# A graph layer's partial sums: sixteen of 37 additions moved from VectorE to a ScalarE copy and an accumulating transfer

## The chip, the core and the metric

The kernel runs on one core of a Trainium2 chip. The metric is the time of one execution on the device in microseconds (us); three runs of the kernel before gave a median of 516.62 us. The profile is of a further execution of its own. TensorE (PE) multiplies matrices into PSUM, VectorE (DVE), ScalarE (ACT) and GpSimd (POOL) work on tiles in SBUF and PSUM, and SyncE (SP) issues transfers. "PEld" is TensorE's loading of weights, which runs beside its matmuls.

## What is computed

A graph layer and then a mixture of experts. The graph layer normalizes the 2,048 rows of x (256 wide), gathers a row for each of 67,584 edges, scales it by the edge's weight, sums the scaled rows by the edge's other end, and adds the sums and a value of each node to x. The experts' layer (eight experts, two for each row) follows and needs all of these sums.

```python
def _L0_gnn_ref(x, values, indices, bias):
    row = indices[0]
    col = indices[1]
    gathered = values[:, None] * x[col]
    out = jax.ops.segment_sum(gathered, row, num_segments=OUT_FEATURES)
    return out + bias
...
edge_index = jnp.stack([src, dst])
x = x + _L0_gnn_ref(_layernorm(x, axis=-1), edge_weight, edge_index, node_vec1)
x = x + _L0_ffn_ref(_layernorm(x, axis=-1)[None], L0_ffn_Wr, L0_ffn_br, L0_ffn_ln_g, L0_ffn_ln_b, L0_ffn_W1, L0_ffn_b1, L0_ffn_W2, L0_ffn_b2)[0]
```

## The kernel before

The kernel turns the edges into a dense matrix of 2,048 x 2,048 and multiplies it by the normalized rows. The rows lie in SBUF in 16 blocks of 128: "acc" holds x and becomes the result, 264 floats a row (256 and eight sums for the later routing); "xn" holds the normalized rows.

The edge loop (a loop over n from 0 to 31, called steps here) makes the dense matrix, 64 columns a step:

- VectorE compares the edges' keys with a counting row: `make_hl` (L330, tile "hl"), `make_eq` (L337, "eq") and `make_hr` (L345, "hr"). It does this one step ahead: step n makes the tiles of step n + 1. "hl" and "hr" have two buffers each.
- `make_cols` multiplies them on TensorE (96 matmuls, L369) into two PSUM tiles "pa" a step, out of a pool of three, and ScalarE copies each to "ar" (L372). SP sends "ar" to a tensor "ad" in DRAM and, after every second step, reads the finished block back as "ac" (L373, L376).
- From step 8 on, `dense` (L383) multiplies finished blocks by the normalized rows, for one pair of row blocks a step, into a PSUM tile "py1" out of a pool of two. The blocks come in groups, `GROUPS`: blocks 0 to 2 for steps 8 to 15, blocks 3 to 6 for steps 16 to 23, blocks 7 to 10 for steps 24 to 31. Blocks 11 to 15 follow after the loop.
- `add` (L388) adds the pair of one step to "acc" in the step after it, on VectorE, after that step's "hl", "eq" and "hr".

Every fourth step a new window of edges is prepared. At steps 1, 5, 9, 13, 17 and 21 `get_win` computes an index on VectorE (L239, L240) and GpSimd gathers three windows (L244, "win_s", "win_d", "win_w"), and, up to step 13, `get_run` another piece of the list (L225, "run"). At steps 4, 8 and so on up to 24 `turn_keys` transposes keys "f" on TensorE (L295, L300), ScalarE copying each before the next (L296, L302). `next_part` splits the weights further two steps later (VectorE L321, ScalarE L322). `X_WORK` is a list of ScalarE's work on x with the step of each item: squares (L429), normalizing (L449) and adding the node values (L454); it ends at step 14. `count_before` (L234) and `scale_dst` (L282) are ScalarE's too.

All of this is inside `tc.manual_schedule`: the instructions of each engine stay in the order in which they are written, so the order within a step is the one of the loop's body. An engine that waits for a semaphore holds up all that stands behind it. Each of GpSimd's transfers is written by GpSimd itself, in its order.

These lines of the loop's body set the order around the change:

```python
elif n % 4 == 1 and q + 2 < GQ:
    get_win(q + 2)
    if q + 4 < GQ:
        get_run(q + 4)
...
for p in late:
    add(*p)
late = []
make_cols(n, *hots.pop(n))
g, k = divmod(n - NB // 2, NB // 2)
if g >= 0:
    late.append(dense(GROUPS[g], 2 * k))
```

Of the kernel before, what the change touches and what calls it, by code (L numbers as in the profile page):

```python
# [10 lines left out]
F32 = mybir.dt.float32  # L11
# [4 lines left out]
OP = mybir.AluOpType  # L16
# [6 lines left out]
P = 128  # L23
# [4 lines left out]
def kernel(  # L28
# [30 lines left out]
    nc = tc.nc  # L59
# [3 lines left out]
    NB = N // P  # L63
# [23 lines left out]
    DX = D + NE  # L87
# [11 lines left out]
    acc = consts.tile([P, NB, DX], F32, name="acc")  # L99
# [11 lines left out]
    pool = lambda name, bufs, **k: edges.enter_context(tc.tile_pool(name=name, bufs=bufs, **k))  # L111
# [148 lines left out]
    hotl = pool("hotl", 2)  # L260
    hotr = pool("hotr", 2)
    rowsp = pool("rowsp", 3)
    ps_k = pool("ps_k", 1, space=PSUM)
    ps_a = pool("ps_a", 3, space=PSUM)
    two = lambda t, g, n: t[:, g * GH:(g + 1) * GH, None, :].to_broadcast([P, GH, n // 2, 2])
# [120 lines left out]

    def add(b, pa):
        nc.vector.tensor_add(acc[:, b:b + 2, :], acc[:, b:b + 2, :], pa[:, :, :DX])  # L388

    ads, acs = {}, {}  # L390
    ET = mybir.EngineType
    ALL = {ET.DVE, ET.Pool, ET.PE, ET.Activation, ET.SP}
    with tc.manual_schedule(engines=ALL):
# [104 lines left out]
        for n in range(NH):  # L498
# [22 lines left out]
            if n in (5, 9, 11):  # L521
                b = {5: 4, 9: 8, 11: 12}[n]
                scales_x(slice(b, b + 4))
            if n in (6, 10, 12):
                b = {6: 0, 10: 4, 12: 8}[n]
                weigh_n(slice(b, b + (8 if n == 12 else 4)))
            for p in late:
                add(*p)
            late = []
            make_cols(n, *hots.pop(n))  # L530
            g, k = divmod(n - NB // 2, NB // 2)
# [58 lines left out]
        for p in range(NA // 2):  # L590
            late.append(dense(GROUPS[3], 2 * p))
            add(*late.pop(0))
        add(*late.pop(0))
    edges.close()

# [7 lines left out]
    with tc.If(n_used < E):  # L603
# [15 lines left out]
        with tc.tile_pool(name="any", bufs=2) as anyp, tc.tile_pool(  # L619
            name="ps_any", bufs=2, space=PSUM  # L620
# [544 lines left out]
    with ExitStack() as nest:  # L1165
        for u in range(SURE - 2, len(whole)):
            s = whole[u]
# [46 lines left out]
```

## Time and profile before

| | |
|---|---|
| median of three runs | 516.62 us (516.45 to 517.64) |
| profiled execution, its own time | 517.81 us |
| its span, first to last instruction | 516.0 us |
| mean granted TensorE clock | 0.967 |
| busy: PE, DVE, ACT, POOL | 460.1, 280.2, 198.5, 153.0 us |
| additions on VectorE (L388) | 37, 25.8 us busy, 700 ns each |
| edge loop with block matmuls (L383 beside L369) | about 74 to 206 us of the span |

A page of the profile gives the busy time of each engine and its groups of instructions. Idle time before a group is put down to what ended it. The busy shares are means over the whole span; a stage is read from its own stretch, and the timeline gives the start and length of the instructions in it. In the timeline, instructions of one kind in a row are merged ("x2"), and what is in brackets is the idle time before and what ended it. The clock column is the share of full TensorE clock that was granted.

### The profile page before, as it was taken

Reading aid. Unit: us, or ns where it says so; the run is one execution under the profiler, and the core shown is the slowest. Engines: PE = TensorE matmul, PEld = TensorE weight load, DVE = VectorE, ACT = ScalarE, POOL = GpSimd, SP = SyncE. Lnnn points to the kernel's source line nnn. Section 1 sums busy time; section 2 is a strip of 40 time slices with the busy share of each in tenths; the row PEclk is TensorE's granted clock in tenths of the full one; section 3 lists DMA queues with packets and bytes.
Section 4 is the critical chain, followed back from the end, with each engine's and each line's share of the span. In section 5 each row is a group of like instructions: output and inputs, shape, how many; then the busy total and the mean of one; then the engine's idle time right before and its main releaser. Section 6 shows DMA issues by size and latency. Waiting matters only on the chain.

```text
span 516.0 us, 12139 instructions
## 1 busy us (share of the span) xinstructions
PE 460.1 (89%) x4996; PEld 390.7 (76%) x4996; DVE 280.2 (54%) x582; ACT 198.5 (38%) x479; POOL 153.0 (30%) x127
## 2 busy tenths in 40 slices
PE   0665898888999999989999999999999999997993
PEld 0454676667877787878887888888888888886882
DVE  5979499999999994247847222243333222121011
ACT  2456386673323321048382332323333333332220
POOL 5470205060330000000142444544343344422231
PEclk9978589999999999999999999999999999999898
DMA  7345556877666566893513996799998667739420
GB/s 230 90 152 140 165 180 215 247 247 211 193 201 207 193 203 191 283 316 109 176 52 83 304 337 199 219 355 375 344 334 287 175 174 214 214 71 332 133 99 31
DMA packets 87684, 106.82 MB, mean 207 GB/s; under 512 B 8656, under 2 KB 77376, under 8 KB 85504
## 3 DMA queue, kind: packets, MB, share of 16 engines
q1 hardware_dynamic: 78576, 91.03, 54.5%
q0 software_dynamic: 7952, 13.77, 11.4%
q10 hardware_dynamic: 1088, 1.09, 0.6%
q8 instruction: 44, 0.72, 0.5%
q14 instruction: 24, 0.20, 0.1%
HBM read 79.85 MB, written 28.14 MB: 209 GB/s over the span
## 4 chain that ended last, share of the span: by engine, by line
PE 43%; DMA 10%; issue 1%; DVE 1%; SPq 0%; POOL 0%; POOLq 0%; DVEq 0%
PE py L1045 17%; PE ph L1031 17%; DMA xs<-xr_d,to_i 7%; PE py L383 4%; PE px L858 2%; DMA out<-y_d 1%; PE px L996 1%; DMA y_rows<-out,to_i 1%; DMA out<-ys,to_i 0%; SPq L1183 0%; PE listed L839 0%; POOL out L1066 0%; POOLq L1210 0%; DVE in_hi L831 0%; DVE in_lo L825 0%
## 5 line engine op out<-in xcount | busy, mean ns | idle before, releaser
L1031 PE MATMUL ph<-xeT,w 128*128 128x256 f32 (+1 forms) x576 | 123.9, 372 | 5.7 <-PEq L1171 4.1
L1031 PEld LDWEIGHTS ph<-xeT,w 128*128 128x128 f32 x576 | 105.1, 192 | 20.6 <-issue 7.2
L1045 PE MATMUL py<-w,hT 128*128 128x256 f32 x544 | 120.6, 379 | 0.0
L1033 ACT ACTIVATE hT<-ph,ec 128x256 f32<-128x256 f32 (+1 forms) x144 | 65.7, 461 | 137.6 <-PE ph L1031 80.1
L1045 PEld LDWEIGHTS py<-w,hT 128*128 128x128 f32 x544 | 102.0, 190 | 13.2
L383 PE MATMUL py<-xn_lo,ac 128*128 128x264 f32 x352 | 85.6, 396 | 0.0
L1053 POOL DMA_INDIRECT y_d<-ys,to_i x30 | 48.9, 1630 | 115.1 <-DVE ys L1048 81.1
L330 DVE TENSOR_TENSOR hl<-k,iota_b 128x4096 bf16<-128x4096 bf16 x32 | 73.1, 2285 | 9.4 <-PE pa L369 9.1
L383 PEld LDWEIGHTS py<-xn_lo,ac 128*128 128x128 f32 x352 | 65.5, 192 | 12.7 <-ACT xn_lo L449 0.2
L369 PE MATMUL pa<-hl,hr 128*32 128x128 bf16 x3072 | 59.4, 234 | 12.2 <-DVE hr L345 6.3
L369 PEld LDWEIGHTS <-hr 128*32 128x32 bf16 x3072 | 49.8, 104 | 24.7 <-issue 14.6
L1048 DVE SCALAR_TENSOR_TENSOR ys<-py,wt,b2w 128x256 f32<-128x256 f32 x34 | 16.4, 484 | 80.6 <-PE py L1045 66.1
L345 DVE TENSOR_TENSOR hr<-eq,w 128x3072 bf16<-128x3072 bf16 x32 | 56.3, 1758 | 2.0 <-ACT w L322 0.5
L963 POOL DMA_INDIRECT xs<-xr_d,to_i x40 | 41.8, 1044 | 52.4 <-DVE r L729 32.8
L1005 DVE TENSOR_SCALAR xeT<-px,ec 128x256 f32<-128x256 f32 (+1 forms) x38 | 18.4, 526 | 63.4 <-PE px L996 55.5
L372 ACT COPY ar<-pa 128x512 f32<-128x512 f32 x64 | 35.6, 585 | 38.6 <-PE pa L369 26.6
L244 POOL DMA_INDIRECT win_s<-in_src,at_i x8 | 11.7, 1458 | 94.7 <-DVE at_i L240 46.2
L388 DVE TENSOR_TENSOR acc<-acc,py 128x528 f32<-128x528 f32 x37 | 25.8, 700 | 22.2 <-PE py L383 22.2
L383 PE MATMUL py<-xn_hi,ac 128*128 128x264 f32 x160 | 36.2, 387 | 1.4 <-DVEq L603 1.4
L383 PEld LDWEIGHTS py<-xn_hi,ac 128*128 128x128 f32 x160 | 30.2, 190 | 6.8 <-issue 1.8
L1020 ACT ACTIVATE b2w<-b,wt 128x256 f32<-128x256 f32 x36 | 16.3, 499 | 27.8 <-DVE wt L1018 25.6
L337 DVE TENSOR_TENSOR eq<-k,iota_b 128x1024 bf16<-128x1024 bf16 x32 | 21.9, 685 | 0.0
(208 smaller groups left out, 331.4 us busy)
## 6 DMA issues: line engine op xcount, KB each, us to landing
w<-in_L_ffn_W SPq DMA_DIRECT2D x44, 1024.0 KB
ad<-ar SPq DMA_DIRECT2D x32, 512.0 KB
ac<-ad SPq DMA_DIRECT2D x16, 1024.0 KB
b<-in_L_ffn_b SPq DMA_DIRECT2D x22, 128.0 KB
out<-y_d SPq DMA_DIRECT2D x4, 512.0 KB
xr_d<-rec SPq DMA_DIRECT2D x1, 1300.0 KB
y_d<-acc SPq DMA_DIRECT2D x1, 1280.0 KB
acc<-in_x SPq DMA_DIRECT2D x2, 512.0 KB
```

The lines of the kernel that those rows point to most:

```text
L330: nc.vector.tensor_tensor(hl.rearrange("p g (n t) -> p g n t", t=2), two(k2[:, 0], g, P), pair(P), OP.is_equal)
L337: nc.vector.tensor_tensor(eq.rearrange("p g (n t) -> p g n t", t=2), two(k2[:, 1], g, RK), pair(RK), OP.is_equal)
L345: nc.vector.tensor_tensor(hr.rearrange("p g i (n t) -> p (g i) n t", t=2), eq[:, :, None, :].to_broadcast([P, GH, 3, RK]), w[:, :, None, : ...
L369: nc.tensor.matmul(pa[j * RK:(j + 1) * RK, m, :], hr[:, g, i, :], hl[:, g, :], start=(i == 0), stop=(i == 2), tile_position=(0, j * RK))
L372: nc.scalar.copy(ar[:, m0:m0 + 4, :], pa)
L383: nc.tensor.matmul(pa[:, i, :DX], acs[c][:, b + i, :], xn(c), start=(c == blocks[0]), stop=(c == blocks[-1]))
L388: nc.vector.tensor_add(acc[:, b:b + 2, :], acc[:, b:b + 2, :], pa[:, :, :DX])
L963: nc.gpsimd.indirect_dma_start(out=(sets[s.set][0] if into is None else into)[:, t, :], out_offset=None, in_=(xr_d if rows is None else ro ...
L1031: nc.tensor.matmul(ph, w1[:, k, c * P:(c + 1) * P], xeT[:, k, :], start=(k == 0), stop=(k == KD - 1))
L1033: nc.scalar.activation(hT[:, c, :s.n * P], ph, AF.Gelu, bias=ec[:, c:c + 1], scale=1.0)
L1045: nc.tensor.matmul(py, hT[:, c, t * P:(t + 1) * P], w2[:, c, :], start=(c == 0), stop=(c == KH - 1))
L1053: st = nc.gpsimd.indirect_dma_start(out=y_d[:, :], out_offset=bass.IndirectOffsetOnAxis(ap=tos[s.to][:, t:t + 1], axis=0), in_=ys, in_offs ...
```

## The change

A pool "sums" with two buffers of 128 x 2 x 264 floats is added. A second function, `add_far`, copies the PSUM pair to such a buffer on ScalarE and then issues a transfer from GpSimd that adds the buffer to the rows of "acc" in SBUF. The loop uses it for the pairs that are added at steps 9 to 16 (those of the first group) and at every odd step after; the even steps from 18 on and all additions after the loop keep `add`.

```diff
+    sums = pool("sums", 2)
...
     def add(b, pa):
         nc.vector.tensor_add(acc[:, b:b + 2, :], acc[:, b:b + 2, :], pa[:, :, :DX])
+
+    def add_far(b, pa):
+
+        s = sums.tile([P, 2, DX], F32, name="sum")
+        nc.scalar.copy(s, pa[:, :, :DX])
+        nc.gpsimd.dma_start(acc[:, b:b + 2, :], s, accum_op=OP.add)
...
             for p in late:
-                add(*p)
+                (add_far if n <= NB or n % 2 else add)(*p)
```

## The prediction

> **What bounds the kernel now.** I call a turn n of the edge loop "step n". I read first where the sums stand, then who waits for them. The table of stretches, for steps 9 to 20 (columns: busy us and instruction count of PE, PEld, DVE, ACT, POOL, then clock, DMA share, GB/s):
>
> ```profile
> 80.00:102.00 22.00, 19.80 (x511) 15.75 (x514) 21.69 (x30) 13.74 (x40) 8.55 (x4) 1.00 0.73 216
> 102.00:124.00 22.00, 19.31 (x407) 15.01 (x399) 21.72 (x24) 12.57 (x31) 8.16 (x4) 1.00 0.73 220
> 124.00:146.00 22.00, 21.18 (x438) 17.16 (x424) 21.72 (x24) 7.62 (x19) 5.39 (x3) 1.00 0.78 241
> ```
>
> VectorE has no gap in any of them. TensorE has some in the first two and hardly any in the third: three block matmuls a row block become four at step 16, and from there TensorE is full as well. So what VectorE loses is worth at most TensorE's gaps before step 17. The waits of PE from 80 to 124 us size them:
>
> ```profile
> PE pa L369 <- issue: 1.4, 3, 0.5
> PE pk L295 <- DVE f L276: 1.1, 2, 0.7
> PE pk L300 <- ACT k L296: 0.9, 2, 0.5
> PE pk L295 <- ACT k L296: 0.5, 1, 0.5
> PE pk L295 <- DVE acc L388: 0.5, 1, 0.5
> PE pa L369 <- DVE hr L345: 0.3, 1, 0.3
> ```
>
> Only waits on VectorE can go. In the timeline of PE they are three holes, worked out from start to start: 0.79 us before step 12's transposes, 0.37 before step 16's edge matmuls, 0.47 before step 16's transposes; 1.63 us in all. The row on "acc" is really the round trip through ScalarE (0.46, like its neighbours) and stays; so do the issue gaps. After step 17 I compared, step by step, the end of hr on VectorE with the start of the matmuls that use it: 1.8, 1.6 and 1.3 us at steps 18 to 20, still 1.9 at step 28 and 0.4 at step 31. TensorE always takes it later. The eight sums moved there are worth nothing.
>
> **What is removed.** Sixteen additions leave VectorE, eight at steps 9 to 16 and eight at odd steps 17 to 31. From the timeline of DVE:
>
> ```profile
> 81.93 0.70 DVE L388 TENSOR_TENSOR acc<-acc,py 128x528 f32<-128x528 f32 x1
> 82.54 2.28 DVE L330 TENSOR_TENSOR hl<-k,iota_b 128x4096 bf16<-128x4096 bf16 x1
> ```
>
> Start to start is 0.61 us, so 16 x 0.61 = 9.8 us of VectorE, of which 1.6 us can show in the time.
>
> **What is added on ScalarE.** Sixteen copies of 128x528 from PSUM. The nearest row is the copy of 128x512 from PSUM at L372, 585 ns, so 0.55 to 0.6 us each, 9.3 us in all. ScalarE is busy 13.74 of 22 us; the room hides the copies themselves. But a copy stands ahead of its step's two copies "ar", and those free the PSUM banks of the edge matmuls (three banks, two used a step).
>
> **What is added on GpSimd, and the new wait.** Each copy is followed by one transfer of 128 rows of 2,112 B, issued by GpSimd in order. The pool "sums" has two buffers, and the order of the built program shows that the copy at step 11 waits for the transfer of step 9 to have landed (12 for 10, and so on). At step 9 the three window gathers and the run gather stand ahead of it in GpSimd's queue. Its timeline:
>
> ```profile
> 58.26 0.95 POOL L225 DMA_INDIRECT run<-in_dst,blk_i  x1 [0.30 <-issue]
> ...
> 82.00 0.94 POOL L244 DMA_INDIRECT win_s<-in_src,at_i  x1 [22.79 <-DVE shift L437]
> 83.25 2.40 POOL L244 DMA_INDIRECT win_d<-in_dst,at_i  x1 [0.31 <-ACT ar L372]
> 85.95 2.35 POOL L244 DMA_INDIRECT win_w<-in_edge_weight,at_i  x1 [0.30 <-PE pa L369]
> 88.61 2.86 POOL L225 DMA_INDIRECT run<-in_dst,blk_i  x1 [0.30 <-issue]
> ```
>
> The same run gather took 0.95 us while VectorE stood still (54.6 to 61.0 us) and 2.86 us beside it; each slow one ends some 0.85 us after the end of the VectorE instruction during which it began. The Trainium skill, "SBUF — State Buffer", section "Who interferes with whom", speaks against this: tensor_tensor with both inputs in SBUF takes only the read interface that it shares with GpSimd, and descriptor generation needs the write interface (it calls this inferred). By the rule the four gathers take 0.94 us and a gap of 0.30 each and end at 87.0; by the rows, with VectorE's work 0.61 earlier, at about 90.2. I follow the rows. The first transfer then starts at 90.5; it has the shape of the run gather, so 0.95 to 2.86 us, and inside hr (until 91.8) I get an end at 92.65.
>
> From GpSimd's end to landing, the chain of waits has this near its end, with nothing beside it:
>
> ```profile
> 501.30 0.97 issue
> 502.27 2.77 DMA y_rows<-out,to_i
> ```
>
> That is 3.7 us, for a gather of half the bytes. The skill's "DMA: Bandwidth & Descriptors", section on the anatomy of one DMA, fits 2.0 us plus bytes/436 GB/s, 2.6 us for these 270 KB, from an unloaded fit; here the DMA engines are 73% busy. An accumulating transfer within SBUF has no row. Bounds: 2.6 below, 8 above (twice the row); I take 4.2. Landing: 96.9 us (95.3 to 100.7). By both rules together it would be 87.3 + 0.95 + 2.6 = 90.9.
>
> **What is behind that wait.** ScalarE wants its copy of step 11 when the block matmuls of step 10 end, 89.7 us. Instead it stands until 96.9, and "ar" of step 11 stands behind it:
>
> ```profile
> 90.62 0.59 ACT L372 COPY ar<-pa 128x512 f32<-128x512 f32 x1 [1.28 <-PE pa L369]
> 91.72 0.58 ACT L372 COPY ar<-pa 128x512 f32<-128x512 f32 x1 [0.52 <-PE pa L369]
> ```
>
> The first bank comes free at 96.9 + 0.55 + 0.55 = 98.0. TensorE begins step 12's edge matmuls at 94.0 and wants that bank for their second half at 94.75: it stands 3.25 us. A landing by 93.6 would cost it nothing; that is the point that decides.
>
> Then step 12: its transposes begin at 101.6, but ScalarE has its backlog first (normalizing and biasing 1.85, counting 0.8, the copy, "ar" 1.05) and copies the first key at 103.0, 1.0 us late. The hole of 0.79 us is inside this, so step 13's edge matmuls start 3.25 + 1.0 - 0.79 = 3.5 us later than before. From there to step 17 TensorE saves the two other holes, 0.84: +2.6 at step 17. At step 13 the gathers are ahead of the transfer again: it would be issued near 113 and land near 117.5, and ScalarE wants it at 116.5, with "ar" of step 15 then done at 119.1, just when TensorE wants a bank. I count nothing there. From step 17 two transfers in four steps leave the queue room.
>
> **The clock.** A standing TensorE has been answered with a lower clock in this trace:
>
> ```profile
> 46.00:49.00 3.00, 0.00 (x0) 0.00 (x0) 2.93 (x5) 1.57 (x4) 0.00 (x0) 0.90 0.23 63
> 49.00:65.00 16.00, 12.24 (x175) 9.19 (x179) 9.36 (x13) 6.08 (x17) 3.77 (x4) 0.50 0.57 161
> ```
>
> After 3.5 us of nothing it ran at half clock for 16 us, and after a 2.6 us hole at 27.4 for about 7; the shortest such dip, at 72, lasted 3.4. A hole of 3.25 us near 95 lies between. Half clock for 3.4 us costs 1.7; for 7 us, 3.5; none, 0. I take 1.7.
>
> **What costs nothing, and its cover.** The transfers' 4.3 MB share DMA engines that feed "ac". The tightest is block 6, for step 16: "ar" of step 13 would be ready at 109.4; its write lands about 3.6 us after its issue ("ad" at 105.05, "ac" that waits for it at 108.63), and I estimate 5 for the read back of twice the bytes: 118, against need at 120.6. The cover is 2.6 us; if the transfers slow "ac" by more, TensorE waits there. The later additions to the same rows on VectorE, and the third set of expert weights, whose place in SBUF now follows "sums" and so waits for GpSimd's transfers, come many microseconds after the last landing: nothing.
>
> **Sum.** +2.6 + 1.7 = +4.3 us. The profiled execution took 517.81 us with a span of 516.0; the median of the runs is 516.62, and 1.8 us of the former lies outside the span. The difference is put on the median: 520.9 us.
>
> **The rivals.** (1) Faster: the gathers run as the rule says, or the landing is below 2 us; the first transfer lands by 93.6, no bank is late, and the 1.63 us of holes go: 515.0. Against it, ten of the fourteen gather rows from 82 to 156 us took over 2 us; for it, the quick row of 0.95. (2) A part of the stall, without a clock dip: landing near 95.3 makes it 1.65 us, no key late, the holes saved: +1.65 - 1.63, so 516.6. (3) Accumulating is slow: 8 us to land makes 100.7, the stall 7 us, a second stall of some 4 us at step 15, half clock for 7 us (3.5), 1 us of late keys, less the holes of 1.63: +13.9, 530.5, with a milder form near 525. (4) The change only shifts work: where TensorE is full everywhere, nothing. That holds after step 17 and is in the sum.
>
> **How the numbers follow.** The forecast has 0.66, rival 3 0.11, rival 2 0.08, rival 1 0.15, of which half ends just short of the bound, as its most, 1.63 us, barely exceeds 0.3% (1.55 us, about what a measurement can tell here). So faster 0.08, same 0.15, slower 0.77. The forecast's own range is 518.5 to 524.1 (the stall from 2.5 to 4.6, a landing 0.8 us earlier to 1.3 later; the clock from 0 to 3.5). For 8 in 10 I go down into rival 1 and up into rival 3: 515.8 to 527.
>
> **What would show it.** In the profile after: a wait of ScalarE at the copy of step 11 ended by the transfer, of about 7 us; PE waiting for "ar" inside one step's edge matmuls near 95 us, then a clock below 1; gathers of 2 us and more ahead of the first transfer; DVE with new holes behind "hl", as it waits for matmuls; steps 18 to 31 at the same 5.21 us as before. Wrong would be: no wait at that copy, transfers landing within 2 us, or "ac" the late one.

## The result, and the profile after

The changed kernel takes 530.03 us (median of four runs, 528.04 to 533.61) beside 517.13 us for the kernel before (516.45 to 518.55): a ratio of 1.024, 95% interval 1.021 to 1.027. On another chip, run again, it was 519.28 beside 511.83 us: 1.014, interval 1.010 to 1.018. It is slower, as forecast, but by 12.9 and 7.5 us where the sum said 4.3, and 530.03 lies outside the range. The profiled execution took 528.58 us with a span of 526.8.

The table of stretches for the same windows as in the prediction, in the profile after (columns as there):

```profile
80.00:102.00 22.00, 18.48 (x428) 14.56 (x429) 20.16 (x27) 12.93 (x38) 12.54 (x7) 0.93 0.77 205
102.00:124.00 22.00, 18.30 (x329) 13.66 (x329) 13.26 (x13) 15.06 (x34) 7.54 (x8) 0.83 0.86 231
124.00:146.00 22.00, 19.67 (x443) 15.85 (x442) 17.93 (x20) 8.36 (x20) 5.77 (x6) 1.00 0.84 208
```

VectorE, full before, has nearly 9 us free in the second row, and TensorE, which was to profit, is busy for less of every row than before. The DMA share rose from 0.73 to 0.86 in the second row. The timeline of ScalarE and that of GpSimd have the forecast wait and the queue behind it:

```profile
97.11 0.60 ACT L394 COPY sum<-py 128x528 f32<-128x528 f32 x1 [7.60 <-DMA acc<-sum]
```

```profile
82.30 3.03 POOL L244 DMA_INDIRECT win_s<-in_src,at_i  x1 [23.18 <-DVE rs L443]
...
90.82 2.16 POOL L225 DMA_INDIRECT run<-in_dst,blk_i  x1 [0.30 <-issue]
92.98 1.93 POOL L395 DMA_DIRECT2D acc<-sum  x2
...
107.41 0.95 POOL L244 DMA_INDIRECT win_w<-in_edge_weight,at_i  x1 [0.30 <-issue]
108.66 0.95 POOL L225 DMA_INDIRECT run<-in_dst,blk_i  x1 [0.30 <-issue]
```

Beside VectorE the run gather took 2.16 us; the next one, at 108.66, took 0.95: VectorE then stood still. What TensorE made of it is in its own timeline, steps 12 and 13:

```profile
98.25 0.85 PE L370 MATMUL pa<-hl,hr 128*32 128x128 bf16 x48 [2.53 <-ACT ar L373]
99.03 4.62 PE L384 MATMUL py<-xn_lo,ac 128*128 128x264 f32 x12
...
105.28 0.99 PE L370 MATMUL pa<-hl,hr 128*32 128x128 bf16 x49
106.75 0.26 PE L370 MATMUL pa<-hl,hr 128*32 128x128 bf16 x4 [0.48 <-issue]
...
110.39 0.96 PE L370 MATMUL pa<-hl,hr 128*32 128x128 bf16 x28 [0.45 <-issue]
111.28 5.36 PE L384 MATMUL py<-xn_lo,ac 128*128 128x264 f32 x12
```

Up to 105.28 this is the forecast: a stop of 2.53 us in the second half of step 12's edge matmuls, then twelve block matmuls in 4.62 instead of 2.94 us. Then comes something that the kernel before had in this stretch only three times, 1.4 us in all: in step 13 TensorE stops six times for 0.44 to 0.48 us, with nothing that the profile names ("issue"), and the block matmuls after that run at half clock. Windows of 2 us show the clock column (last but two) and the DMA share beside it:

```profile
100.00:102.00 2.00, 2.00 (x6) 1.57 (x5) 2.00 (x2) 2.00 (x6) 0.00 (x0) 0.50 1.02 240
106.00:108.00 2.00, 0.81 (x22) 0.39 (x14) 0.00 (x0) 1.97 (x7) 1.59 (x2) 1.00 0.98 356
112.00:114.00 2.00, 2.00 (x6) 1.56 (x5) 2.00 (x3) 1.81 (x5) 0.00 (x0) 0.50 1.11 315
```

The start of the edge matmuls, after less before, is 0.8 us late at step 12, 4.3 at step 13, 11.3 at step 14, 8.5 at step 17 and 14.5 at step 31; TensorE's last group starts 14.0 us late. Of that 3.2 come back at the very end: the span ends 6.8 us after GpSimd's last operation before, 3.6 after.

The third place to look is SP's queue. Its waits from 79 to 235 us (total, times, longest), first of the kernel before, then of the changed one:

```profile
SPq L376 <- DMA ad<-ar: 42.0, 12, 5.1
```

```profile
SPq L377 <- DMA ad<-ar: 75.3, 12, 8.3
```

A block's "ac" is issued only when "ad" has landed. That wait nearly doubled, and SP issues in order, so the next "ad" stands behind it. Block 6 shows it, the second "ad" and the "ac" behind it, in SP's timeline before and after:

```profile
105.05 0.36 SPq L373 DMA_DIRECT2D ad<-ar  x1
108.63 0.33 SPq L376 DMA_DIRECT2D ac<-ad  x1
```

```profile
111.99 0.36 SPq L374 DMA_DIRECT2D ad<-ar  x1
117.94 0.33 SPq L377 DMA_DIRECT2D ac<-ad  x1
```

At the end of the loop the last "ac" and, behind it, the experts' weights are late, and VectorE and GpSimd wait for SP at the branch of L610. SP's and VectorE's timelines after:

```profile
225.22 0.33 SPq L377 DMA_DIRECT2D ac<-ad  x1
```

```profile
237.20 0.45 DVE L1094 COPY xs<-none 128x520 f32<-128x520 f32 x1 [2.96 <-SPq L610]
```

In the profile before these were at 207.41 and 221.45 us: SP 17.8 us late, the branch 15.8.

### The profile page after: what moved, and what is told of

The parts are those of the page before. It is cut to its first block, busy times and chain, and to the rows that moved or that the text cites. A ratio compares the mean times of both kernels' runs of the same rounds, so it can differ in the third digit from the quotient of the medians.

```text
span 526.8 us, 12182 instructions
## 1 busy us (share of the span) xinstructions
PE 466.5 (89%) x4996; PEld 395.0 (75%) x4996; DVE 270.7 (51%) x566; ACT 208.0 (39%) x495; POOL 158.8 (30%) x143
## 4 chain that ended last, share of the span: by engine, by line
PE 41%; DMA 9%; issue 2%; DVE 1%; SPq 0%; POOL 0%; POOLq 0%; DVEq 0%
PE py L1052 17%; PE ph L1038 17%; DMA xs<-xr_d,to_i 7%; PE py L384 4%; PE px L865 2%; DMA out<-y_d 1%; PE px L1003 1%; DMA y_rows<-out,to_i 1%; DMA out<-ys,to_i 0%; PE listed L846 0%; SPq L1190 0%; POOL out L1073 0%; POOLq L1217 0%; DVE in_hi L838 0%; DVE in_lo L832 0%
## 5 line engine op out<-in xcount | busy, mean ns | idle before, releaser
L384 PE MATMUL py<-xn_lo,ac 128*128 128x264 f32 x352 | 88.8, 407 | 0.0
L1060 POOL DMA_INDIRECT y_d<-ys,to_i x30 | 48.9, 1630 | 113.5 <-DVE ys L1055 76.7
L370 PE MATMUL pa<-hl,hr 128*32 128x128 bf16 x3072 | 61.7, 236 | 19.7 <-issue 12.1
L384 PEld LDWEIGHTS py<-xn_lo,ac 128*128 128x128 f32 x352 | 67.7, 198 | 13.7 <-issue 0.2
L370 PEld LDWEIGHTS <-hr 128*32 128x32 bf16 x3072 | 50.9, 105 | 33.4 <-issue 25.2
L395 POOL DMA_DIRECT2D acc<-sum x16 | 14.5, 927 | 77.7 <-ACT sum L394 77.7
L244 POOL DMA_INDIRECT win_s<-in_src,at_i x8 | 14.1, 1768 | 72.0 <-DVE rs L443 45.7
L389 DVE TENSOR_TENSOR acc<-acc,py 128x528 f32<-128x528 f32 x21 | 14.6, 700 | 20.9 <-PE py L384 20.9
```

Of the source, the lines that this page charges most:

```text
L370: nc.tensor.matmul(pa[j * RK:(j + 1) * RK, m, :], hr[:, g, i, :], hl[:, g, :], start=(i == 0), stop=(i == 2), tile_position=(0, j * RK))
L384: nc.tensor.matmul(pa[:, i, :DX], acs[c][:, b + i, :], xn(c), start=(c == blocks[0]), stop=(c == blocks[-1]))
L1060: st = nc.gpsimd.indirect_dma_start(out=y_d[:, :], out_offset=bass.IndirectOffsetOnAxis(ap=tos[s.to][:, t:t + 1], axis=0), in_=ys, in_offs ...
```

## The experiments

Two theories at first. Queue theory: the wait of ScalarE stops TensorE, and the rest follows from the stop. Fetch theory: the transfers' traffic delays TensorE's own instructions. A third, DMA theory, came out of the first four runs: the transfers take so much of the DMA engines' time that the edge blocks' own transfers fall behind. The table gives, for every profile on the four later chips, the start of the edge matmuls of steps 17 and 31, the issue of the last "ac", the start of TensorE's last group, the time from the end of GpSimd's last operation to the end of the span, and the ratio of the times to those of the kernel before on the same chip.

| run | step 17 | step 31 | last "ac" | last PE | end | ratio (95%) |
|---|---|---|---|---|---|---|
| b0_before | 116.76 | 193.22 | 199.20 | 492.15 | 6.8 | 1.0005 (0.9989 to 1.0022) |
| a0_after | 122.87 | 205.23 | 214.69 | 504.40 | 3.6 | 1.0137 (1.0098 to 1.0175) |
| e1_bufs4 | 120.62 | 198.26 | 212.98 | 504.80 | 3.6 | 1.0192 (1.0166 to 1.0218) |
| e9_order | 121.20 | 200.47 | 214.17 | 506.36 | 3.6 | 1.0176 (1.0105 to 1.0246) |
| e2_first | 121.10 | 198.48 | 205.98 | 498.64 | 3.0 | 1.0070 (1.0048 to 1.0091) |
| e7_first4 | 124.77 | 202.72 | 209.79 | 502.17 | 3.0 | 1.0050 (1.0019 to 1.0080) |
| e3_late | 117.11 | 194.46 | 204.20 | 493.55 | 3.0 | 0.9941 (0.9916 to 0.9967) |
| e5_load | 119.46 | 197.97 | 204.42 | 497.07 | 3.2 | 0.9998 (0.9973 to 1.0022) |
| e6_spare_acc | 122.00 | 201.58 | 212.59 | 501.75 | 3.6 | 1.0091 (1.0061 to 1.0121) |
| d_twice | 120.96 | 199.06 | 210.71 | 500.47 | 4.3 | 1.0128 (1.0068 to 1.0188) |
| e8_few4 | 117.45 | 195.88 | 203.22 | 495.87 | 7.0 | 1.0029 (1.0011 to 1.0047) |
| e10_gpadd | 119.52 | 197.57 | 204.70 | 497.38 | 6.8 | 1.0060 (1.0037 to 1.0083) |
| e4_drop | 115.03 | 193.33 | 200.37 | | 7.0 | not comparable |
| c_pad | 116.44 | 192.89 | 200.39 | 493.22 | 6.8 | 0.9996 (0.9975 to 1.0016) |

The times in the first four expectations start from the first chip's 517 us; on these chips the kernel before takes 511.07 to 511.83, so that 5.6 us are to be taken off them. One profile is one execution, and its times are held against those of b0_before, whichever of the four chips it ran on. c_pad, whose loop is that of the kernel before, ends 1.1 us later at "last PE", so about 1 us there is chance.

**Four buffers (e1_bufs4).**

```diff
-    sums = pool("sums", 2)
+    sums = pool("sums", 4)
```

> Edit: four buffers in sums instead of two, so that ScalarE's copy of a step waits for the transfer of four steps before. Queue theory (the wait for the first transfer's landing stops ScalarE, then TensorE at step 12; the lower clock and the slow step 13 follow from that stop): the 7.6 us wait at the copy of step 11 and the 2.5 us wait of PE for ar are gone, clock 1.00 from 80 to 124 us, step 17 begins within 2 us of before; about 4 to 5 us of later gaps stay, so near 521. Fetch theory (the transfers' traffic delays TensorE's own instructions, seen as PE waiting for issue inside the edge matmuls): the stop of about 3 us goes but the issue gaps of step 13 and later stay: near 526.

Measured: ratio 1.0192. ScalarE no longer waits for a transfer, steps 13 to 16 start every 4.3 to 4.8 us without a stop, and step 16 begins 1.0 us earlier than in the kernel before. Then TensorE waits for block 6, and the loop's end for SP. Timelines of PE and of DVE:

```profile
115.07 3.93 PE L384 MATMUL py<-xn_lo,ac 128*128 128x264 f32 x10 [3.79 <-DMA ac<-ad]
```

```profile
225.38 0.45 DVE L1094 COPY xs<-none 128x520 f32<-128x520 f32 x1 [7.75 <-SPq L610]
```

Neither theory has it. By the queue theory 4 us should have been left (521 from 517); 9.4 were. That is the fetch theory's size, but its "issue" gaps are only 1.6 us here. The last "ac" is 13.8 us late, the branch follows it at 12.4 us, and TensorE's last group is 12.7 us late although step 31 was only 5.0 late.

**One group alone (e2_first, e3_late).** The condition of `add_far` is cut to `n <= NB`, or to `n > NB and n % 2`.

> Edit: only the eight sums of steps 9 to 16 are copied and transferred; all later ones stay on VectorE. Queue theory: the whole stop is still there, so step 17 begins about 8 us later than before, and nothing is added after it: near 525. Fetch theory: the same up to step 17, and the issue gaps of 4 to 5 us after step 18 are gone because their transfers are: also near 525. Told apart only together with the next run: the two halves should add up to the whole.

> Edit: only the eight sums at odd steps 17 to 31 are copied and transferred. Queue theory: no copy waits for a transfer and TensorE is full there, so nothing changes: 516.5 to 517.5. Fetch theory: the PE waits for issue inside the edge matmuls after step 18 are 4 to 5 us longer than before: near 521.

Measured: 1.0070 and 0.9941. The first group alone has the queue's stop (ScalarE 10.9 us in two waits, TensorE 3.2 us) and loses 5.3 us up to step 31. The late group costs the loop 1.2 us. Its lower time is no gain of the loop: its last PE group is 1.4 us late, and an end that is 3.8 us shorter more than pays for that. The queue theory had expected no change, the fetch theory a loss of 4 us; of the first group they had expected a loss of 8, and it was 3.9.

**Traffic without dependence (e5_load), accumulating traffic (e6_spare_acc), twice the plain traffic (d_twice).** In all three VectorE keeps its additions, and the copied sums, in four buffers, go to spare tiles that nobody reads.

```diff
     def add_far(b, pa):
...
-        nc.gpsimd.dma_start(acc[:, b:b + 2, :], s, accum_op=OP.add)
+        t = spare.tile([P, 2, DX], F32, name="spare_t")
+        nc.gpsimd.dma_start(t, s)
+        add(b, pa)
```

e6 adds `accum_op=OP.add` and uses four zeroed tiles in turn; d_twice issues the plain transfer twice, to two of five tiles.

> Edit: VectorE keeps all its additions; beside them the sixteen copies are made into four buffers and sent by plain transfers (no accumulation) to four spare tiles of the same size that nothing reads. The result is the same as before. Queue theory: with four buffers nobody waits, VectorE is as before, so 517 to 518. Fetch theory: the traffic is there, so the PE waits for issue grow by 4 us or more: 521 or more. If accumulating transfers are what is dear, and not any transfer, this one is near 517 while the four-buffer version is not.

> VectorE keeps all of its additions. Beside them ScalarE copies the sixteen sums as in the changed kernel, with four buffers, and GpSimd issues sixteen accumulating transfers, but onto four spare tiles that nobody reads. It differs from the run with plain transfers to spare tiles (ratio 1.000) only in that the transfers accumulate, and from the changed kernel with four buffers (ratio 1.019) only in that no addition depends on them. DMA theory (an accumulating transfer takes the engines for about twice the time of a plain one, so that the edge blocks' own two transfers fall behind): 9 us above the kernel before, 1.018, the block-6 wait of the step-16 dense pair back at 3 to 4 us. Dependency theory (what costs is that rows are brought in late): as the plain transfers, 1.000 within 0.003. Anything between gives the share of each.

> VectorE keeps all additions; each of the sixteen copied sums is moved to spare tiles twice, by two plain transfers. A plain one took 0.7 us of each DMA engine in the run with one each, an accumulating one 1.5 us, so that two plain ones stand for one that accumulates. Engine-time theory: as the accumulating transfers to spare tiles, step 31 at 201 to 202 (8.4 us above the kernel before), a wait for block 6 of about 2 us at step 16, ratio 1.009. If accumulating itself is what slows the others: as one plain transfer each, step 31 near 198, no wait for block 6, ratio 1.000.

The DMA queues from 60 to 230 us (packets, MB, share of 16 engines), of e5_load, e6_spare_acc and d_twice:

```profile
q0 software_dynamic: 1906, 5.93, 9.8%
```

```profile
q0 software_dynamic: 2928, 5.92, 17.0%
```

```profile
q0 software_dynamic: 3184, 10.25, 16.3%
```

The kernel before has 3.3% there. In 170 us that makes packet time of (9.8% - 3.3%) x 170 / 16 = 0.69 us on every DMA engine for a plain transfer, 1.46 for an accumulating one of the same bytes. Two plain ones take 1.38. The loss follows that time, not the accumulating: "last PE" is 4.9 us late with one plain transfer, 9.6 with an accumulating one, 8.3 with two plain ones, and the last "ac" 5.2, 13.4 and 11.5. e5 hides its 4.9 us, 3.6 of them behind the shorter end, so that it measures as no change. e6 measures 1.009, between its two forecasts of 1.018 and 1.000, and its wait for block 6 is 1.83 us, not 3 to 4. No run has the sixteen copies without transfers. A straight line through the two plain runs (4.9 and 8.3 us late) leaves some 1.5 us for no transfer at all, an estimate not far above chance.

**The sums dropped (e4_drop).** `add_far` is replaced by nothing.

> The sixteen sums are neither copied, transferred nor added: they are left out of the result, which also changes the routing behind the loop, so that only the edge loop's steps are to be read. It is the most that freeing VectorE can bring there. From the idle time before the edge matmuls of steps 12 and 16 in the profile before: step 17 begins 1.6 us earlier than in the kernel before, and steps 18 to 31 run at the same 5.2 us each, so that step 31 begins 1.6 us earlier. If VectorE bounded the loop as a whole, step 31 would be up to 9.8 us earlier.

Step 17 begins 1.73 us early, as the holes had said (1.6). Step 31 begins 0.1 us late: at step 18 an "issue" gap of 1.40 us took most of it back, with no added transfer in the program. So such gaps are not the transfers' alone, and even a VectorE relieved at no price gives the loop next to nothing.

**The pair again (b0_before, a0_after).**

> The kernel before, unchanged, run again for its trace beside the others on one chip. Its steps are the yardstick: step 17 at 123.6 us and step 31 at 200.4 in the first profile. Open: the variants so far ended 3.0 to 3.6 us after GpSimd's last operation, the first profile of this kernel 6.75 us. If that tail belongs to this kernel's program, it is 6.75 again here and the 3 us that the late-only variant gained lie behind the loop; if it is a chance of one execution, it is near 3.5 here, and the variants' gains and losses lie in the loop.

> The changed kernel, unchanged, run again for its trace beside the others. Queue theory (ScalarE's second copy waits for a transfer, TensorE stops, and falls to half its clock): the 7.6 us wait at step 12 and the late second half of step 12 return, and account for no more than 4 of the 13 us; 1.024 of the kernel before. Instruction theory (TensorE's own instructions come late while the transfers fill the DMA engines): step 13 again takes over 9 us with gaps of 0.4 to 0.5 us that no semaphore ends, and such gaps sum to about 7 us more than before. If step 13 is short here, those gaps are no fixed part of the change.

Step 12 repeats: ScalarE waits 8.36 us for the transfer, TensorE 4.14 us for "ar", and step 13 begins 5.6 us late. The six gaps in step 13 do not (step 14 begins 4.5 us after step 13). They may be the difference between the two chips: step 13 took 4.3 us in the kernel before and 11.3 in the first profile after, 7.0 more, and the loss on the first chip is 5.4 us larger. One profile on each can't show it. But other gaps come: five of 0.6 to 1.7 us, 5.9 in all, four of them after step 17. They have favourite places. After the 86th of step 14's 96 edge matmuls TensorE stopped in the kernel before and in eight of its variants. Timelines of PE, of b0_before and of e8_few4:

```profile
100.30 0.34 PE L369 MATMUL pa<-hl,hr 128*32 128x128 bf16 x10 [0.43 <-issue]
```

```profile
101.40 0.34 PE L370 MATMUL pa<-hl,hr 128*32 128x128 bf16 x10 [2.40 <-issue]
101.68 4.62 PE L384 MATMUL py<-xn_lo,ac 128*128 128x264 f32 x12
```

It was 0.43 us in three programs without early transfers (b0_before, c_pad, e3_late), 0.71 in e4_drop and 0.88 to 2.40 in five with them; in four others with them (e1_bufs4, e7_first4, e9_order, d_twice) and in e10_gpadd, which has none, it did not stop, so that traffic alone does not set it. After 2.40 the block matmuls ran at half clock. The Trainium skill, "Runtime: NRT & Kernel Launch", section "Instruction fetch mechanics", has instructions fetched in blocks of 16 KiB by a DMA queue of the engine's own, and calls the cost of a boundary mostly hidden. The page of every profile here has a queue of that kind, 44 packets and 0.72 MB, 16 KB each, and the times of its packets in the traces settle what these stops are. In all fourteen profiles of the table the 87th edge matmul of step 14 comes behind the same packet of that queue, the twelfth, and never less than 1.2 us after that packet's end. Four of them:

| run | the packet | 87th matmul | after the packet's end | stop before it |
|---|---|---|---|---|
| b0_before | 97.88 to 98.84 | 100.30 | 1.46 | 0.43 |
| a0_after | 104.54 to 105.55 | 106.95 | 1.40 | 1.31 |
| e8_few4 | 99.20 to 100.18 | 101.40 | 1.22 | 2.40 |
| e1_bufs4 | 97.70 to 98.92 | 100.77 | 1.85 | none |

From step 8 to the end of the loop these profiles have 43 "issue" stops of over 0.3 us, and every one ends 1.2 to 1.6 us after such a packet. By this timing TensorE waits there for its next block of instructions, as the fetch theory has it, and the cost is not always hidden: the five stops of a0_after make 5.9 us. What makes a block late is open. In the five programs with early transfers and a stop, the twelfth packet began 4.8 to 5.9 us after step 13 did, in the four with early transfers and no stop 1.6 to 3.1, in the five others 3.2 to 4.0. The six stops of the first profile are something else: the last packet before them had ended 8.9 us before the first of them was over. They stay unexplained.

**The transfer ahead of the gathers (e9_order).** Two buffers, but `get_win` and `get_run` moved behind the loop over `late`.

> The changed kernel with two buffers as it is, but in steps 9, 13 and 17 the far sum's copy and transfer are issued ahead of the step's gathers, so that the transfer no longer stands behind 10 us of gathers in GpSimd's queue. Queue theory: the third copy finds its buffer free, ScalarE's 7.6 us wait at step 12, TensorE's 4.1 us stop and the half clock after it are gone, steps 9 to 12 run as in the variant with four buffers (step 13 at 94.8 instead of 99.7). DMA theory: what the four-buffer variant still lost stays, so that block 6 is again about 3.8 us late at step 16, step 17 begins near 120.6 and the ratio is 1.014 to 1.019. If GpSimd's queue was not the cause of the wait, step 13 begins at 99.7 again.

TensorE's stop for "ar" is gone, as the queue theory says: step 13 begins at 95.26 instead of 99.73, step 16 at 108.23 as with four buffers. ScalarE still waits, 4.2 us at step 12 and 7.9 at step 16, where a key comes 2.3 us late. Block 6 is 3.7 us late, SP holds the branch (6.5 us), and the ratio stays at 1.018: the DMA theory's part.

**First group, four buffers (e7_first4).** Condition `n <= NB`.

> Only the first group's eight sums go the far way, with four buffers. Up to step 17 it is the four-buffer variant: block 6 about 3.8 us late at step 16, step 17 at 120.6. If the chain of the edge blocks' transfers stays behind only as long as transfers are added, it catches up by the end: no wait at the branch, step 31 at 197 to 198, and with eight transfers the short end: ratio about 1.002 to 1.006. If the first group's transfers alone hold the chain behind for good, the last block's transfer is issued near 213 as with sixteen, the branch waits 7 us, and the ratio is 1.019.

The waits of PE from 72 to 232 us have:

```profile
PE py L384 <- DMA ac<-ad: 8.9, 1, 8.9
```

The 3.8 us of e1 became 8.9, so that step 17 missed its forecast by 4 us. The runs scatter: 18 reached from 509.1 to 521.7 us, and their median lies 5.3 us above that of the kernel before, twice what the ratio of 1.005 makes, so that the size of this loss is uncertain. Block 6 is where a small delay decides. As forecast, SP catches up once no more transfers come: the last "ac" 7.1 us after step 31 begins (14.7 in e1, 6.0 in the kernel before), no wait at the branch.

**A version that might beat both (e8_few4, e10_gpadd).** Only the sums handed over in steps 10, 11, 14 and 15, four buffers; in e10 GpSimd adds them itself (`nc.gpsimd.tensor_tensor`), with no transfer.

> Only four sums take the way round by ScalarE and an accumulating transfer, those handed over in steps 10, 11, 14 and 15, in the two pile-ups; four buffers. DMA theory: a quarter of the added load, so that the wait for block 6 at step 16 (3.8 us with sixteen) falls under 1 us, step 17 begins between 115.2 (the 1.7 us that dropping the sums gave) and 117.7, and with the 3.1 us shorter end that every variant showed the ratio is 0.991 to 0.996. If the first far sums alone bring on the loss, step 17 begins near 120.6 as with sixteen, ratio 1.00 or above.

> The same four sums are copied by ScalarE as before, but GpSimd adds them to the rows itself, from SBUF to SBUF: no transfer at all. If DMA load is what cost, the whole gain of a freed VectorE shows: step 17 at 115.1 (1.7 us early) and the ratio 0.991 to 0.994 with the shorter end. If GpSimd's additions hold up VectorE, its hl, eq and hr operations beside them are longer than 2.29, 0.68 and 1.76 us, and step 17 is not before 116.8. GpSimd stands with the gathers of step 13, so a far sum of steps 14 and 15 may also come late; then the next step's addition or copy waits for it.

Neither does: 1.003 and 1.006. e8 lost to the gap shown above what it had gained (step 14 began 0.9 us early, step 15 2.5 us late). In e10, GpSimd and VectorE timelines of the same microseconds:

```profile
84.26 2.57 POOL L395 TENSOR_TENSOR acc<-acc,sum 128x528 f32<-128x528 f32 x2
```

```profile
84.12 4.33 DVE L346 TENSOR_TENSOR hr<-eq,w 128x3072 bf16<-128x3072 bf16 x1
```

VectorE's "hr" takes 1.76 us alone and 4.33 beside GpSimd's two additions: the 2.57 us that they last. It agrees with the Trainium skill, "SBUF — State Buffer", section "Who interferes with whom", by which tensor_tensor with both inputs in SBUF contends with GpSimd's reads.

**Instructions without transfers (c_pad).**

> The kernel before with all its additions on VectorE; where the changed kernel has a far sum, ScalarE copies one column of constants to a spare column and GpSimd sets a spare column three times: 16 and 48 instructions of about 0.1 us that nothing waits for, and no transfer. In every variant so far the program ended 3.0 to 3.6 us after GpSimd's last operation, in two executions of the kernel before 6.8 us. If that depends on the program's instructions only, the end is 3.6 here too and the ratio 0.994, with the loop's step 31 within 0.5 us of 193.2. If it comes with the added transfers, the end stays 6.8 and the ratio is 1.000.

1.000, and the end stays at 6.8 us. The shorter end comes with transfers in GpSimd's ring: 3.0 to 4.3 us in every profile with eight or more, 6.8 to 7.0 in every one with none or four. Why is open.

## Why the prediction was right and wrong

- **What bounds the loop, and the most that can be gained: right.** The holes came to 1.63 us; dropping the sums gave 1.73 at step 17 and nothing at step 31.
- **Gathers beside VectorE: the rows were right, the rule was not.** 2.16 to 3.03 us beside VectorE, about 1 us where it stood still.
- **The landing: right by two errors.** 96.9 was forecast and 97.11 measured. The transfers' start was 92.98, not 90.5, but from the first one's end (half of the merged 1.93 us) to landing it was 3.2 us, not 4.2. On the second chip that way took 6.2 us, so that the near hit is luck. (Twice the 3.7 us of the row is 7.4, not 8.)
- **The stop and the clock: right.** TensorE stood 2.53 us (4.14 on the second chip) against 3.25, and half clock cost 4.62 - 2.94 = 1.68 us against 1.7. The key was not late. Step 13 was forecast 3.5 + 1.7 = 5.2 us late; it was 4.3 and 5.6. That the clock fell is no rule: after a stop of 3.21 us at the same place (e2_first) it did not.
- **"What costs nothing, and its cover": the step that failed.** The 4.3 MB were held against a 2.6 us cover of block 6 and left at zero. Each transfer's packets took 1.46 us on every DMA engine, of which I had no row. Block 6's write, put at 3.6 us, took 5.9 in the first profile after and 9.4 in e1, and its block came up to 8.9 us late in the variants. Worse, the cover was worked out for one block: on SP's in-order queue a late "ad" holds the next, so that the delay stays while transfers come, and ends in the experts' weights and the branch. Copies and accumulating traffic alone, without the queue's wait and without any addition depending on them, put step 31 8.4 us late and the last group 9.6 (e6). I had named the sign ("TensorE waits there") and given it no chance and no width.
- **How the loss divides in the changed kernel itself** is shown in part. On the second chip step 31 is 12.0 us late, 6.1 of it by step 17 (forecast: 2.6 + 1.7 = 4.3), and the branch 13.6, where VectorE waits 2.3 us for SP. SP's chain can hold the branch nearly that long by itself: in e1 step 31 is only 5.0 us late and the branch 12.4. On the first chip 7.0 of step 31's 14.5 us came in step 13, with the six stops and the half clock behind them, and the cause of these stops stays open.
- **"Steps 18 to 31 at the same 5.21 us": wrong.** From step 17 to step 31 it was 76.5 us in the kernel before and 82.4 in the changed one on the second chip (76.7 and 82.8 on the first), 4.6 of the added 5.9 us being "issue" gaps, waits for blocks of instructions. The gaps had been seen and put down as fixed.
- **"At step 15 … I count nothing": right** in the first profile, where TensorE was late itself; the next wait for a transfer (1.84 us, step 16) cost nothing. TensorE's lateness is luck here.
- **The sum against the time** left out the end, which is 3.2 us shorter and makes the loss look smaller than it is: TensorE's last group is 12.3 us late on the second chip, the median 7.5.
- **Rival 3** had the size, by luck, but not the way: landings of 6 to 8 us after the start of the issue were seen in the later profiles, yet the accumulating cost through engine time and SP's queue.

## What to carry to other kernels

An added transfer is paid for by those who already use the DMA engines: compute engine time for each transfer, then follow the tightest in-order chain of loads to its end, not only to the next consumer. Read how full the resource taken into use is as carefully as that of the one relieved: VectorE was full here and worth 1.7 us, the DMA engines 73% busy and worth 9.6 at the last group (e6). An idle time that the profile puts down to "issue" may be a wait for the engine's next block of instructions: look for the packet of its queue just before. Where several causes lie in one loop, removing one (e1, e9) only shows the next.

## What the runs showed of the hardware

- The packets of an accumulating transfer of 270 KB within SBUF take 1.46 us on each of the 16 DMA engines, those of a plain one 0.69, with 64 packets more each (2,928 against 1,906 for sixteen). Packet times can overlap: the DMA share of 2 us reached 1.11 here.
- TensorE stops with no semaphore behind it, at recurring instructions, for 0.4 to 2.4 us. In the fourteen later profiles each such stop of over 0.3 us in the loop ends 1.2 to 1.6 us after a 16 KB packet of the instruction queue has landed; the six stops of the first profile's step 13 do not.
- The length of a stop did not decide alone whether the clock was halved (for 3.4 us or longer). It was after stops of 2.07 (e5), 2.40 (e8), 3.79 (e1) and 4.14 us (a0), and some 2 us after stops of 1.46 (d_twice) and 1.58 us (e6); it was not after 1.83 (e6) and 3.21 (e2).
- The end of the program after GpSimd's last operation is 3.0 to 4.3 us with eight or more added transfers in GpSimd's ring, 6.8 to 7.0 with none or four; not explained.
